# A two-layer transformer on one core: block 0 normalised a layer early, roots moved, logits before results, evictions spread

## The chip, the cores and the metric

The kernel runs on one core of a Trainium2 chip. The core has TensorE (PE, matrix products; PEld are its weight loads), VectorE (DVE), ScalarE (ACT), GpSimd (POOL) and SyncE (SP, which here only issues DMAs). Each engine works through its own queue in order; engines wait for one another by semaphores. The metric is device time in microseconds (us), the median of three runs.

## The reference, cut to what matters

The input x has 4 sequences of 512 tokens with 256 features. Two layers follow, each with attention and a feed-forward part; each part gets a layernorm of x and is added to x.

```python
x = x + attn0(layernorm(x))   # 16 heads of 16, causal, softmax over 512 keys
x = x + ffn0(layernorm(x))    # every output feature picks 2 of 8 experts
x = x + attn1(layernorm(x))   # 16 query heads, 4 kv heads of 128
x = x + ffn1(layernorm(x))    # 4-bit weights, gelu gate, 256 -> 2048 -> 256

def ffn0(h):                                  # h: tokens x 256
    logits = (h @ router_w.T + router_b)      # tokens x 256 x 8
    w, sel = top_k(softmax(logits), 2); w = w / w.sum()
    c = zeros(tokens, 8).at[sel].add(w)       # expert weights, summed over features
    out = einsum('th,eoh->teo', h, expert_w) + expert_b
    return einsum('te,teo->to', c, out)
```

attn1 sees the reshaped array as a sequence axis of 4 and a batch of 512, so its scores are small; four groups of kv heads share the queries four to one. ffn1 unpacks two 4-bit codes from each byte, looks up their values and multiplies by a scale for 32 of them.

## The kernel before, in words

The 2048 tokens lie in SBUF as 16 groups of 128 (`xres`), four groups making a block; there are four blocks. All products are in fp32; a product of 512 columns over 256 features is four matmul instructions.

**The planner.** The order on PE, DVE and POOL is the program's order (in layer 1 that of ACT too; in layer 0 a scheduler orders ACT by its own estimate). The program finds the order as it is written: work off the main line is held in `streams`, generators that yield `need(engine, cost, gap, cond)` before each piece. Between pieces of the main line, `fill` (L140) opens a *slot*: it gives PE and DVE budgets in estimated us, first issues what was deferred, then goes through the streams from the front and lets each issue pieces while the engine's budget is above zero, its condition holds and `gap` slots have passed since its last piece. `defer` (L134) puts off an ACT instruction to the next slot, so that it stands behind other work.

**Layer 0** (the first 421 us). Attention runs in 32 batches: scores, maxima on DVE, a shift of the queries, exponentials on ACT, mixing, and a division (`divided`, L731) with two transposes and two output products per block. Two slots per batch are filled with streams: the norm and projections of the next block (`prepare`), and the feed-forward part. That part has, per group: four *logit* products (`logit_pieces`, L298), 17 steps of *weights* on DVE with a tanh and sums on ACT (`weight_pieces`, L371; the tanh and its follower are `lesser`, L404), four *result* products (`result_pieces`, L318) whose outputs ACT multiplies by the expert weights, and *additions* to `xres` on DVE (`addition_pieces`). `hidden_pieces` (L281) normalises and transposes a block for them. Logits and results are let through by how far the weights are (`made()`). The streams stand in the order fold, additions, weights, results, logits. About half of the feed-forward part of layer 0 is left when layer 1 starts, and is filled into layer 1's attention.

**A norm** (`norm_pieces`, L187) takes statistics of four groups on DVE, an inverse square root by a guess on DVE and ten small steps (`rsqrt_steps`) on POOL or DVE, and writes the normalised `xn` on DVE; where POOL makes the steps, `xn` is held back two slots. Only one norm is under way at a time (`normed`). Four transposes per half follow on PE, and ACT copies them to `xT`.

**Layer 1's attention** (from 421 us). `wqkv` and `wpj` are loaded on SP's queue when layer 0's memory is free. `start_pieces(j)` (L908) normalises block j, transposes it and makes the values; block 0's must be complete before the first round, the others are streams. A round p takes one kv head of one block: five projections (`project1`, four of queries and one of keys), scores, softmax on DVE, `mix` (L999: values mixed, four accumulators copied to `oT` by ACT), four output products `output` (L1017). The rounds are interleaved: the projections of round p+1, with mixing of round p ahead of the third, then the outputs of p with scores and softmax of p+1 between. After each piece `between` (L1070) fills a slot. Its PE budget follows `share`, the layer-0 products still left spread over the slots up to round 8; from round 9 it is 0.2.

```python
def between(dve=None):
    fill(PE=1.9 * share + 0.2, DVE=dve or 2.7 * share + 1.4)
...
for h in range(HPK + 1):
    if h == 2 and p >= 0:
        mix(p)
    if new:
        project1(p + 1, h)
        between()
```

PE's small outputs share two PSUM buffers (`ps_dn`, tag `dn`): projections, products, transposes, values. Each is free again when ACT has copied it.

Once layer 0's last addition is issued, 4-bit weights are unpacked by `dequant_pieces` (L833) in the remaining rounds: DVE steps, and two ACT instructions, `over` (L855) and `sign` (L860).

**Layer 1's feed-forward part** (from about 883 us) is untouched by the change.

Of the kernel before, what the change touches and what calls it, by code (L numbers as in the profile page):

```python
# [32 lines left out]
def tile_transformer(  # L33
# [97 lines left out]
    streams = []  # L131
    deferred = []

    def defer(emit):  # L134

        deferred.append((slot, emit))

    left = {"PE": 0.0, "DVE": 0.0}

    def fill(**budget):  # L140

        nonlocal slot
        slot += 1
        while deferred and deferred[0][0] < slot:
            deferred.pop(0)[1]()
        for engine, b in budget.items():
            left[engine] = min(left[engine], 0.0) + b
        again = True
        while again:
            again = False  # L150
            for stream in list(streams):
                while stream.ready(left):
                    engine, cost = stream.go()
                    left[engine] -= cost
                    again = True
                if stream.next is None:
                    streams.remove(stream)
# [26 lines left out]

    normed = []

    def norm_pieces(j, pool, small, out, deinterleave=False, eng=None, cond=None):  # L187

        yield need("DVE", 1.0, cond=lambda: not normed and (cond is None or cond()))
        normed.append(j)  # L190
        st = small.tile([P, 4, 6], F32, tag="ln_st", name=f"ln_st{j}")
        mv = small.tile([P, 4, 2], F32, tag="ln_mv", name=f"ln_mv{j}")
        rs = small.tile([P, 4], F32, tag="ln_rs", name=f"ln_rs{j}")
        for t in range(4):
            if t == 2:
                yield need("DVE", 1.0)
            nc.vector.bn_stats(st[:, t, :], xres[:, 4 * j + t, :])
            nc.vector.bn_aggr(mv[:, t, :], st[:, t, :])
        eng = eng or nc.gpsimd
        yield need("DVE", 0.6 if eng is nc.gpsimd else 2.6)  # L200
        v = rsqrt_guess(rs, mv[:, :, 1], small, j)
        rsqrt_steps(eng, rs, v, small, j)
        xn = pool.tile([P, 4, HID], F32, tag="xn", name=f"xn{j}")
        for t in range(4):
            if t % 2 == 0:
                yield need("DVE", 0.9, 2 if not t and eng is nc.gpsimd else 0)
            src, dst = xres[:, 4 * j + t, :], xn[:, t, :]
            if deinterleave:
                src = src.rearrange("p (k two) -> p two k", two=2)
                dst = dst.rearrange("p (two k) -> p two k", two=2)  # L210
            nc.vector.tensor_scalar(
                dst, src, mv[:, t, 0:1], rs[:, t : t + 1], ALU.subtract, ALU.mult
            )
        out.append(xn)
# [66 lines left out]
    def hidden_pieces(b):  # L281

        out = []
        done = (4 * b - 5, 1)
        yield from norm_pieces(b, b1, b2, out, cond=lambda: b < 2 or done in halves)
        xT = b2.tile([P, 2, 512], F32, tag="xT", name=f"xT{b}")
        for hc in range(2):
            yield need("PE", 0.5, 1 - hc)
            ps = transposed(out[0], hc, ps_dn, "dn", f"xT_ps{b}_{hc}")
            ps = ps.rearrange("p t q -> p (t q)")  # L290
            if hc:
                nc.scalar.activation(xT[:, hc, :], ps, AF.Identity, bias=last_16)
            else:
                nc.scalar.copy(xT[:, hc, :], ps)
        normed.clear()
        xTs[b] = xT
# [74 lines left out]
    def weight_pieces():  # L371

        tt, stt = nc.vector.tensor_tensor, nc.vector.scalar_tensor_tensor
        for g in range(NT):
            yield need("DVE", 1.25, cond=lambda: g in logits and logits[g][1] < slot)
            d = logits[g][0]
            hi4 = b1.tile([P, 4, HID], F32, tag="hi4", name=f"hi4_{g}")
            lo4 = b1.tile([P, 4, HID], F32, tag="lo4", name=f"lo4_{g}")
# [1 line left out]
            gap = b1.tile([P, HID], F32, tag="gap", name=f"gap_{g}")  # L380
            th = b1.tile([P, HID], F32, tag="th", name=f"th_{g}")
            w1 = b1.tile([P, HID], F32, tag="w1", name=f"w1_{g}")
            c1 = b2.tile([P, NE], F32, tag="c1", name=f"c1_{g}")
            sums = b2.tile([P, NE + 1], F32, tag="sums", name=f"sums_{g}")

            tt(hi4, d[:, 0:4], d[:, 4:8], ALU.max)
# [17 lines left out]
            def lesser(th=th, gap=gap, w1=w1):  # L404
                nc.scalar.activation(th, gap, AF.Tanh, scale=0.5)
                nc.scalar.activation(w1, th, AF.Identity, bias=half_t, scale=0.5)

            defer(lesser)
            for e in (0, 4):
                yield need("DVE", 1.25)  # L410
                tt(  # L411
# [3 lines left out]

            yield need("DVE", 0.7, 1)
            owing = b5.tile([P, HID], F32, tag="owing", name=f"owing_{g}_")
            nc.vector.tensor_scalar(gap, gap, 0.0, -1.0, ALU.is_equal, ALU.mult)  # L420
            stt(owing, th, -1.0, gap, ALU.add, ALU.add)
# [19 lines left out]
            stt(c1, sums[:, :NE], 0.5, c1, ALU.mult, ALU.add)  # L441
            weights[g] = c1, slot
            del logits[g]

# [6 lines left out]
    with ExitStack() as l0:  # L451
# [333 lines left out]
        for piece in prepare(0):  # L785
# [3 lines left out]
        mask(0)  # L789
        fold = Stream(fold_pieces())  # L790
        streams += [
            fold, Stream(addition_pieces()), Stream(counted(weight_pieces())), Stream(result_pieces()),
            Stream(logit_pieces()),
        ]
        for n in range(NBT):
            j, s, gs = batches[n]
# [28 lines left out]
            if n in (2, 6):  # L825
                load_x(n // 4 + 2)
        mixed(NBT - 1)
        last = Stream(divided(*batches[NBT - 1][:2]))
        streams.insert(0, last)
        while last.next is not None:  # L830
# [2 lines left out]
    def dequant_pieces(pool, once, n, packed, scales, to, defer=defer):  # L833

        wi = pool.tile([P, 2, HID], I32, tag="dq_w", name=f"dq_w{n}")
        sc = pool.tile([P, 2, HID], F32, tag="dq_s", name=f"dq_s{n}")
        for i in range(2):  # L840
            nc.sync.dma_start(out=wi[:, i], in_=packed[i])
            for b in range(8):
                nc.sync.dma_start(out=sc[16 * b : 16 * b + 16, i], in_=scales[i](b))
        mi = once.tile([P, 2, 2, HID], I32, tag="dq_m", name=f"dq_m{n}")
        si = once.tile([P, 2, 2, HID], I32, tag="dq_i", name=f"dq_i{n}")
        a = once.tile([P, 2, 2, HID], F32, tag="dq_a", name=f"dq_a{n}")
        over = once.tile([P, 2, 2, HID], F32, tag="dq_b", name=f"dq_b{n}")
# [7 lines left out]
        defer(lambda: nc.scalar.activation(over, mi, AF.Relu, bias=minus_12, scale=2.0))  # L855
        yield need("DVE", 0.9)
        ts(si[:, :, 0], wi, 8, None, ALU.bitwise_and)
        ts(si[:, :, 1], wi, 4, 8, ALU.logical_shift_right, ALU.bitwise_and)

        defer(lambda: nc.scalar.activation(sign, si, AF.Identity, bias=half_t, scale=-0.125))  # L860
        yield need("DVE", 1.25)
        stt(a, mi, 4.0, mi, ALU.max, ALU.add)
        yield need("DVE", 1.25, 1)
        stt(a, a, -4.0, over, ALU.add, ALU.add)
        yield need("DVE", 1.25)
        tt(a, a, sign, ALU.mult)
        yield need("DVE", 1.3)
        tt(to, a, sc.unsqueeze(2).to_broadcast([P, 2, 2, HID]), ALU.mult)
# [16 lines left out]
    with ExitStack() as l1:  # L885
# [14 lines left out]
        def into_T(out, to, name):  # L900

            for hc in range(2):
                yield need("PE", 0.5, 1 - hc)
                ps = transposed(out[0], hc, ps_dn, "dn", f"{name}_ps{hc}")
                nc.scalar.copy(to[:, hc, :], ps.rearrange("p t q -> p (t q)"))
            normed.clear()

        def start_pieces(j):  # L908

            out = []  # L910
            yield from norm_pieces(j, c1, c1, out, cond=lambda: (4 * j + 3, 1) in added)
            xT = c2.tile([P, 2, 512], F32, tag="xT", name=f"xT1_{j}")
            yield from into_T(out, xT, f"xT1_{j}")
            v = c2.tile([P, 4, NKV, P], F32, tag="v", name=f"v{j}")
# [84 lines left out]
        def mix(p):  # L999
# [10 lines left out]
                    )  # L1010
            oT = c2.tile([P, HPK, 512], F32, tag="oT", name=f"oT{p}")
            oq = oT.rearrange("p h (t c q) -> p c t h q", c=NC, q=32)
            for c in range(NC):
                nc.scalar.copy(oq[:, c], avs[c])
            state["o"] = oT

        def output(p, t):  # L1017

# [54 lines left out]
        for p in range(-1, NP):  # L1073
# [22 lines left out]
            for h in range(HPK + 1):  # L1096
                if h == 2 and p >= 0:
                    mix(p)
                    if not new:
                        first_products()  # L1100
                if new:
                    project1(p + 1, h)
                    between()
            for t in range(4):
                if p >= 0:
# [20 lines left out]
    with ExitStack() as f1:  # L1126
# [9 lines left out]
        def inner(j):  # L1136
            xT = normed_T(j, d2, d2, ps_dn, "dn", deinterleave=True) if j else x_first
            it = d2.tile([P, NJ, 2, 512], F32, tag="it", name=f"it{j}")
            for jj in range(NJ):
# [21 lines left out]
                if j < 2 and jj % 4 == 3:  # L1161
                    at = 4 * j + 2 * (jj // 4)
                    for _ in dequant_pieces(
                        d2, d1, f"d{at}", [down_w[at + i] for i in range(2)],
                        [
                            lambda b, i=i: down_s[at + i, b : b + 1, :].to_broadcast([16, HID])
                            for i in range(2)
                        ],
                        wd[:, at : at + 2], lambda emit: emit(),
                    ):  # L1170
                        pass
            return it
# [85 lines left out]
```

## Time and profile before

| what | value |
|---|---|
| median of three runs | 1235.4 us (1234.69 to 1236.05) |
| profiled execution | 1231.27 us, span 1229.6 us |
| mean granted TensorE clock | 0.983 |
| PE busy | 1172.0 us (95%), 7278 matmuls |
| DVE busy | 812.5 us (66%), 1862 instructions |
| ACT busy | 483.7 us (39%), 1101 instructions |
| POOL busy | 131.3 us (11%), 249 instructions |
| DMA | 26.78 MB |

The profile is of one execution, a little faster than the median of the three runs. Busy PE time is modelled from pipelined matmuls and overstates the work, so a stall is better read from the starts of neighbouring groups of matmuls. In a line of the timeline stand: start, duration, engine, line and operation, the names written and read, shapes, count, and in brackets the idle time before it with what ended that. "lg_ps" is a logit product, "eo" a result product, "qk_ps" a projection, "xT_ps" a transpose, "v_ps" a value product, "a" the mixing of layer 1, "o" in L1025 its output product, "th" the tanh of the weights.

### The profile page before, as it was taken

To read this page: it belongs to the slowest core of one execution; us is meant where nothing else is said; L and a number is where in the kernel's file an instruction comes from. 1 tells how busy PE (TensorE), PEld (TensorE's weight loads), DVE (VectorE), ACT (ScalarE), POOL (GpSimd) and SP (SyncE) were. 2 spreads that over 40 slices of the span, in tenths; PEclk is the share of its full clock that TensorE was granted. 3 is DMA by queue.
4 is the path that set the end of the run, shared out by engine and by line. 5 is a ranking of instruction groups with operands and counts; after the bars stand their busy time and mean duration, and the time that the engine had idled before them with its cause. 6 is when DMAs were issued, how large, how long until landed. Compare 5 with 4: busy or idle time off the path is not lost.

```text
span 1229.6 us, 18921 instructions
## 1 busy us (share of the span) xinstructions
PE 1172.0 (95%) x7278; PEld 682.0 (55%) x7278; DVE 812.5 (66%) x1862; ACT 483.7 (39%) x1101; POOL 131.3 (11%) x249
## 2 busy tenths in 40 slices
PE   6888999999999897999999999999999999999998
PEld 3666555555545443555555555555645456475487
DVE  3655589887889838395967396588589962734710
ACT  1243455555555533344444344345234431312300
POOL 7343422111121001000000000100000000000000
PEclk9899999999999988999999999999999999999999
DMA  6031102000000310000000001011010000000000
GB/s 201 5 100 35 19 1 36 1 1 2 1 2 2 117 55 1 1 1 1 1 1 1 1 1 35 10 43 53 1 50 19 1 1 17 1 1 18 0 1 35
DMA packets 19386, 26.78 MB, mean 22 GB/s; under 512 B 4992, under 2 KB 13440, under 8 KB 19040
## 3 DMA queue, kind: packets, MB, share of 16 engines
q1 hardware_dynamic: 18624, 24.40, 7.0%
q10 hardware_dynamic: 672, 1.18, 0.4%
q8 instruction: 57, 0.93, 0.3%
q14 instruction: 33, 0.27, 0.1%
HBM read 19.27 MB, written 2.10 MB: 17 GB/s over the span
## 4 chain that ended last, share of the span: by engine, by line
PE 77%; DVE 16%; ACT 3%; DMA 2%; issue 1%; POOL 1%; SPq 0%; ACTq 0%; DVEq 0%; POOLq 0%
PE qk_ps L937 10%; PE y L1178 9%; PE g L874 9%; PE u L874 9%; PE o L1025 8%; PE lg_ps L251 7%; PE eo L251 6%; PE s L633 4%; DVE mx L653 3%; PE s L683 2%; PE v_ps L919 2%; PE qk_ps L548 2%; PE av L719 2%; PE s L950 1%; DVE lg L411 1%
## 5 line engine op out<-in xcount | busy, mean ns | idle before, releaser
L937 PE MATMUL qk_ps<-xT,wqkv 128*128 128x512 f32 x320 | 151.3, 604 | 5.0 <-ACT qT L941 5.0
L251 PE MATMUL lg_ps<-rw,xT 128*128 128x512 f32 x256 | 125.7, 614 | 4.4 <-ACT part L339 1.4
L251 PE MATMUL eo<-ew,xT 128*128 128x512 f32 x256 | 122.8, 605 | 1.9 <-ACT part L339 1.9
L1025 PE MATMUL o<-wpj,oT 128*128 128x256 f32 x512 | 119.4, 382 | 0.0
L653 DVE TENSOR_REDUCE mx<-s 128x1 f32<-128x384 f32 (+3 forms) x176 | 100.4, 632 | 18.3 <-PE s L648 18.3
L1178 PE MATMUL y<-wd,it 128*128 128x256 f32 x512 | 112.1, 379 | 0.0
L1025 PEld LDWEIGHTS o<-wpj,oT 128*128 128x128 f32 x512 | 96.0, 190 | 28.2 <-issue 16.4
L1178 PEld LDWEIGHTS y<-wd,it 128*128 128x128 f32 x512 | 97.0, 190 | 15.6 <-issue 2.9
L937 PEld LDWEIGHTS qk_ps<-xT,wqkv 128*128 128x128 f32 x320 | 59.7, 192 | 75.3 <-issue 61.8
L692 ACT ACTIVATE pt<-s 128x512 f32<-128x512 f32 (+1 forms) x176 | 83.7, 561 | 35.7 <-PE s L683 35.6
L874 PE MATMUL g<-xT,wgu 128*128 128x512 f32 x192 | 90.5, 593 | 0.0
L874 PE MATMUL u<-xT,wgu 128*128 128x512 f32 x192 | 90.2, 592 | 0.0
L702 POOL TENSOR_SCALAR_AFFINE_SELECT pt<-pt 128x256 f32<-128x256 f32 (+2 forms) x88 | 56.7, 651 | 267.1 <-ACT pt L692 266.7
L339 ACT ACTIVATE part<-eo,c 128x256 f32<-128x256 f32 x128 | 53.7, 472 | 78.9 <-PE eo L251 78.9
L1156 ACT ACTIVATE th<-sq 128x512 f32<-128x512 f32 x64 | 40.3, 630 | 88.6 <-DVE sq L1155 88.6
L251 PEld LDWEIGHTS eo<-ew,xT 128*128 128x128 f32 x256 | 47.6, 193 | 48.5 <-issue 40.9
L251 PEld LDWEIGHTS lg_ps<-rw,xT 128*128 128x128 f32 x256 | 46.7, 194 | 49.8 <-issue 38.4
L633 PE MATMUL s<-qk 32*128 32x128 f32 (+3 forms) x512 | 67.0, 496 | 2.6 <-ACT pt L692 1.9
L239 DVE TENSOR_TENSOR xres<-xres,y 128x256 f32<-128x256 f32 x16 | 6.7, 420 | 91.3 <-PE y L1178 91.3
L313 ACT COPY lg<-lg_ps 128x512 f32<-128x512 f32 x64 | 37.7, 589 | 71.2 <-PE lg_ps L251 71.2
L366 DVE TENSOR_TENSOR part<-part 128x512 f32<-128x512 f32 x32 | 21.9, 684 | 65.5 <-ACT part L339 65.4
L941 ACT COPY qT<-qk_ps 128x512 f32<-128x512 f32 x64 | 37.8, 593 | 61.4 <-PE qk_ps L937 61.4
(254 smaller groups left out, 1820.2 us busy)
## 6 DMA issues: line engine op xcount, KB each, us to landing
qk<-stage SPq DMA_DIRECT2D x56, 64.0 KB, 2.4
wqkv<-in_w_qkv SPq DMA_DIRECT2D x2, 1536.0 KB, 8.3
rw<-in_router_w SPq DMA_DIRECT2D x8, 256.0 KB, 4.6
ew<-in_expert_w SPq DMA_DIRECT2D x8, 256.0 KB, 4.8
wpj<-in_w_proj SPq DMA_DIRECT2D x1, 2048.0 KB, 15.4
out<-xres SPq DMA_DIRECT2D x4, 512.0 KB, 2.6
xres<-in_x SPq DMA_DIRECT2D x3, 512.0 KB, 7.1
dq_wgu<-in_gate_w SPq DMA_DIRECT2D x8, 128.0 KB, 2.4
```

What stands on the lines that cost most here:

```text
L251: nc.tensor.matmul(ps, lhsT=xT[:, hc, (g % 4) * P : (g % 4 + 1) * P], rhs=w[:, hc, 2 * pair : 2 * pair + 2, :].rearrange("p e o -> p (e o) ...
L339: nc.scalar.mul(part[:, e % 4], ps[:, i], c[:, e : e + 1])
L633: nc.tensor.matmul(tiles[h][:, b * nk : (b + 1) * nk].rearrange("p (c k) -> p c k", k=P), lhsT=queries(j, g)[r, s], rhs=qk[r, g, : j + 1, ...
L653: nc.vector.tensor_reduce(maxes[n % 2][:, :nb, h, 0], ps[:, : nb * nk].rearrange("p (b k) -> p b k", b=nb), AX.X, ALU.max,)
L692: nc.scalar.activation(pt[:, i, : nb * nk], tiles[2 * pair + i][:, : nb * nk], AF.Exp, scale=0.25)
L702: nc.gpsimd.affine_select(out=last, in_=last, compare_op=ALU.is_ge, fill=0.0, base=0, pattern=pattern, channel_multiplier=-1,)
L874: nc.tensor.matmul(ps, lhsT=wgu[:, w, half, jj, par * P : (par + 1) * P], rhs=xT[:, half, :], start=half == 0, stop=half == 1,)
L937: nc.tensor.matmul(ps, lhsT=wqkv[:, hc, kv, h, :], rhs=xT[:, hc, :], start=hc == 0, stop=hc == 1,)
L941: nc.scalar.copy(kT if h == HPK else qT[:, h, :], ps)
L1025: nc.tensor.matmul(ys[t // 2][:, t % 2], lhsT=state["o"][:, h, t * P : (t + 1) * P], rhs=wpj[:, HPK * kv + h, :], start=kv == 0 and h == 0 ...
L1156: nc.scalar.activation(th, sq, AF.Tanh, scale=0.7978845608028654)
L1178: nc.tensor.matmul(ps, lhsT=it[:, c // 2, c % 2, t * P : (t + 1) * P], rhs=wd[:, c // 2, c % 2, :], start=c == 0, stop=c == 2 * NJ - 1,)
```

## The change

- Deferral gets a number of slots (one, as before, by default). The tanh of the weights and the `sign` of the dequantisation are deferred by two. The weights' next step waits until the tanh has been issued, the multiplication by `sign` waits a slot.
- In the streams, logits stand in front of results. The weights of group g wait for the results of group g-5; their outputs `c1` have five buffers instead of two.
- Layer 0's norm of block 3 (`hidden_pieces`) makes its roots on DVE, and its first transpose waits two slots after `xn` instead of one.
- Layer 1's norm of block 0 is issued in layer 0's tail, with the roots on DVE; layer 1 begins with its transposes, two slots later. The other blocks of layer 1 keep their roots on POOL; `xn` is held back three slots, the first transpose two.
- Of the four copies of mixing to `oT`, one follows mixing and one each of the three projections after it (in the last round all four follow mixing).

```diff
-    def defer(emit):
-        deferred.append((slot, emit))
+    def defer(emit, slots=1):
+        deferred.append((slot + slots, emit))
...
-        while deferred and deferred[0][0] < slot:
-            deferred.pop(0)[1]()
+        for due in [d for d in deferred if d[0] <= slot]:
+            deferred.remove(due)
+            due[1]()
...
-    def norm_pieces(j, pool, small, out, deinterleave=False, eng=None, cond=None):
+    def norm_pieces(j, pool, small, out, deinterleave=False, eng=None, cond=None, wait=2):
...
-                yield need("DVE", 0.9, 2 if not t and eng is nc.gpsimd else 0)
+                yield need("DVE", 0.9, wait if not t and eng is nc.gpsimd else 0)
...
-        yield from norm_pieces(b, b1, b2, out, cond=lambda: b < 2 or done in halves)
+        last = b == NBLK - 1
+        yield from norm_pieces(
+            b, b1, b2, out, eng=nc.vector if last else None,
+            cond=lambda: b < 2 or done in halves,
+        )
...
-            yield need("PE", 0.5, 1 - hc)
+            yield need("PE", 0.5, 0 if hc else 1 + last)
...
-            yield need("DVE", 1.25, cond=lambda: g in logits and logits[g][1] < slot)
+            yield need(
+                "DVE", 1.25,
+                cond=lambda: g in logits and logits[g][1] < slot
+                and (g < 5 or (g - 5, 1) in halves),
+            )
...
-            c1 = b2.tile([P, NE], F32, tag="c1", name=f"c1_{g}")
+            c1 = b5.tile([P, NE], F32, tag="c1", name=f"c1_{g}")
...
                 nc.scalar.activation(th, gap, AF.Tanh, scale=0.5)
                 nc.scalar.activation(w1, th, AF.Identity, bias=half_t, scale=0.5)
+                lessers.append(th)
-            defer(lesser)
+            defer(lesser, 2)
...
-            yield need("DVE", 0.7, 1)
+            yield need("DVE", 0.7, 1, cond=lambda: lessers)
+            lessers.clear()
...
-            fold, Stream(addition_pieces()), Stream(counted(weight_pieces())), Stream(result_pieces()),
-            Stream(logit_pieces()),
+            fold, Stream(addition_pieces()), Stream(counted(weight_pieces())),
+            Stream(logit_pieces()), Stream(result_pieces()),
...
         mixed(NBT - 1)
+        streams.insert(0, Stream(norm_pieces(0, b1, b2, normed_first, eng=nc.vector)))
         last = Stream(divided(*batches[NBT - 1][:2]))
...
-        defer(lambda: nc.scalar.activation(sign, si, AF.Identity, bias=half_t, scale=-0.125))
+        defer(lambda: nc.scalar.activation(sign, si, AF.Identity, bias=half_t, scale=-0.125), 2)
...
-        yield need("DVE", 1.25)
+        yield need("DVE", 1.25, 1)
         tt(a, a, sign, ALU.mult)
...
-                yield need("PE", 0.5, 1 - hc)
+                yield need("PE", 0.5, 0 if hc else 2)
...
-            out = []
-            yield from norm_pieces(j, c1, c1, out, cond=lambda: (4 * j + 3, 1) in added)
+            out = [] if j else normed_first
+            if j:
+                yield from norm_pieces(
+                    j, c1, c1, out, cond=lambda: (4 * j + 3, 1) in added, wait=3
+                )
...
-            for c in range(NC):
-                nc.scalar.copy(oq[:, c], avs[c])
             state["o"] = oT
+            state["a"] = [lambda c=c: nc.scalar.copy(oq[:, c], avs[c]) for c in range(NC)]
+
+        def mixed_out(n):
+            for _ in range(n):
+                state["a"].pop(0)()
...
                     mix(p)
+                    mixed_out(1 if new else NC)
                     if not new:
                         first_products()
                 if new:
                     project1(p + 1, h)
+                    if h >= 2 and p >= 0:
+                        mixed_out(1)
                     between()
```

More of the change, by code (lines that the diff above doesn't have):

```diff
@@ L373, in weight_pieces @@
         tt, stt = nc.vector.tensor_tensor, nc.vector.scalar_tensor_tensor
+        lessers = []
         for g in range(NT):
-            yield need("DVE", 1.25, cond=lambda: g in logits and logits[g][1] < slot)
+            yield need(
[3 more added lines that the diff above has]
+            )
             d = logits[g][0]
@@ L443, in weight_pieces @@
             del logits[g]
+    normed_first = []
     with ExitStack() as l0:
@@ L1168, in inner @@
                         ],
-                        wd[:, at : at + 2], lambda emit: emit(),
+                        wd[:, at : at + 2], lambda emit, slots=1: emit(),
                     ):
```

## The prediction

> **What bounds the kernel now.** First the kernel by stage: busy time of each engine in five stretches (columns: stretch and length in us; busy time and count of PE, PEld, DVE, ACT, POOL; granted PE clock, DMA share, GB/s).
>
> ```profile
> 0.00:421.00 421.00, 385.37 (x3986) 228.36 (x3986) 307.54 (x744) 193.69 (x486) 115.29 (x189) 0.98 0.12 30
> 421.00:492.00 71.00, 59.50 (x194) 26.83 (x193) 44.10 (x133) 27.72 (x66) 8.12 (x30) 0.88 0.20 73
> 492.00:732.00 240.00, 239.76 (x1129) 134.54 (x1128) 157.51 (x389) 106.24 (x280) 2.02 (x10) 1.00 0.00 1
> 732.00:883.00 151.00, 144.86 (x859) 88.17 (x858) 107.23 (x216) 64.42 (x123) 5.89 (x20) 0.99 0.11 29
> 883.00:1229.60 346.60, 342.55 (x1117) 204.09 (x1115) 196.13 (x383) 91.62 (x146) 0.00 (x0) 1.00 0.04 13
> ```
>
> From 492 us on TensorE is the bound: four matmuls of 128x512 (one "product") take 1.72 us wherever nothing disturbs them, and almost nothing is lost. PE's work is the same after the change, so only its lost time can move. I measure a loss as start of a group to start of the next, less the undisturbed time (1.72 us a product, 0.86 us for 8 transposes). Layer 0 loses most, but VectorE's chain of maxima under a fixed budget paces it. What the change touches are single stalls; next the waits of PE that name most of them, then, from the timeline, the seam between the layers, with the landing times of layer 1's weights:
>
> ```profile
> PE xT_ps L227 <- DVE xn L211: 7.8, 3, 3.2
> PE qk_ps L937 <- ACT qT L941: 5.0, 6, 2.1
> ```
>
> ```profile
> 419.84 0.82 SPq L890 DMA_DIRECT2D wqkv<-in_w_qkv  x2
> ...
> 430.83 1.38 DVE L211 TENSOR_SCALAR xn<-xres,ln_mv,ln_rs 128x256 f32<-128x256 f32 x4 [1.22 <-POOL ln_rs L183]
> 431.39 1.76 PE L227 MATMUL xT_ps<-ident,xn 128*128 128x128 f32 x8 [1.84 <-DVE xn L211]
> ...
> 434.72 5.68 PE L919 MATMUL v_ps<-wqkv,xT 128*128 128x512 f32 x7 [1.56 <-ACT xT L905]
> ```
>
> ```profile
> DMA to landing us min/median/max: 6.6/8.3/10.0
> ```
>
> PE waits for a normalised block, then for its copies; the second half of the weights lands at 420.2 + 10.0 = 430.2, unnoticed. Next ScalarE as the culprit (timeline, then clock by stretch):
>
> ```profile
> 735.68 1.88 PE L251 MATMUL eo<-ew,xT 128*128 128x512 f32 x4
> ...
> 736.22 0.42 ACT L405 ACTIVATE th<-gap 128x256 f32<-128x256 f32 x1 [2.77 <-DVE gap L401]
> ...
> 737.08 2.03 ACT L1014 COPY oT<-a 128x512 f32<-128x512 f32 x4
> ...
> 738.98 0.62 ACT L941 COPY qT<-qk_ps 128x512 f32<-128x512 f32 x1
> ...
> 739.65 3.50 PE L937 MATMUL qk_ps<-xT,wqkv 128*128 128x512 f32 x4 [2.09 <-ACT qT L941]
> ```
>
> ```profile
> 735.70:744.90 9.20, 7.11 (x14) 2.79 (x13) 8.57 (x26) 5.80 (x17) 0.00 (x0) 0.81 0.00 0
> 786.00:793.00 7.00, 5.27 (x16) 2.42 (x15) 3.08 (x4) 4.38 (x8) 3.13 (x7) 1.00 0.00 1
> ```
>
> A tanh that waits for VectorE and four mixing copies stand in front of the copy PE needs. Last, what follows a round's fifth projection today:
>
> ```profile
> 857.68 1.89 PE L1025 MATMUL o<-wpj,oT 128*128 128x256 f32 x8
> ...
> 857.88 0.59 ACT L941 COPY kT<-qk_ps 128x512 f32<-128x512 f32 x1 [1.59 <-PE qk_ps L937]
> 858.36 1.15 ACT L855 ACTIVATE dq_bgu<-dq_mgu,minus 128x1024 f32<-128x1024 int32 x1
> ```
>
> The output products o start with no gap, because the oT copies were done long before. The next ACT instruction starts 0.48 us after the kT copy.
>
> **The change part by part.**
>
> *A. Block 0 normalised in layer 0's tail.* Loss at the seam: 427.67 to 431.39 less 1.72 is 2.0; transposes 431.39 to 434.72 less 0.86 is 2.5; values 434.72 to 444.10 less 6.88 is 2.5 (clock 0.74 there): 7.0. After, three products precede the transposes instead of five (two slots instead of a whole norm), so they stand at 426.0, and the values want both weight halves: SP still issues them behind layer 0's last o (L764), so they land at 430.2. The values end at 430.2+0.86+5.16, plus one half-clock stretch (1.7) for an idle PE: 438.0 against 444.1, with 2 products (3.4) still to do. Gain 2.7; ends 0 (a longer half clock) and 4.4 (none). The norm's 6 us on DVE (4 x 0.59 statistics, 0.6 guess, 10 x 0.16 roots, 4 x 0.35) take slots that the weights had; DVE even idles 3.3 us there before the add at 406.2. Without that cover the divisions of the tail would come up to 2 us later. Its ten POOL roots leave POOL.
>
> *B. Block 3 of layer 0, roots on DVE, transposes a slot later.* Loss 461.36 to 465.65 less 0.86, 465.65 to 467.53 less 0.86, 467.53 to 470.72 less 1.72: 3.4+1.0+1.5 = 5.9. All roots now lie on the queue that also writes xn, and two slots (3.4 us each here) cover the rest. Gain 5.5 (ends 0, 5.9).
>
> *C. Later blocks of layer 1, one slot more before xn and before the transposes.* Block 1: 477.33 to 483.75 less 3.44, then 2.4 and 1.85: 7.2. POOL's chain (478.64 to 483.16) gets a slot more. Gain 6.5 (ends 0, 7.2).
>
> *D. Tanh two slots later, in layer 1.* 735.68 to 739.65 less 1.72 is 2.25; the next product at half clock loses 1.57. Gain 3.8 (ends 0, 3.8). Behind the new wait stand the owing step and all later DVE work; the steps before it end about 5 us after the tanh today in layer 0, a slot is 3.7 us, so I add nothing (at most the 0.93 us of both activations in 16 groups, were the cover gone).
>
> *E. The same in layer 0.* The tanhs at 240.11 and 312.93 (2.3 and 2.8 us of waiting) hold back the exponentials whose score buffers PE wants: 2.70 and 2.75 us for 8 score matmuls against 1.07 at 272.02. That is 3.3; I take 3.0, as ACT's order in layer 0 is set elsewhere (ends -2, 3.9).
>
> *F. Dequantisation's sign later, evictions interleaved.* Stalls after 780: 787.03 to 789.36 (1.9), the values at 802.7 (1.6), two of 0.4. I take 2.5 of 4.3 (ends 0, 4.3); the copies stay on ACT.
>
> *G. Mixing's evictions spread.* In place of four oT copies after mixing comes one, then one after each of the projections 2, 3 and 4. The o products need all four (each copy carries a quarter of the queries of every o), and the last is now behind the kT copy, which waits for projection 4. From 857.68: kT copy from 857.88, oT from 858.36 to 858.96, and weights to load again (0.19): 1.4 us in which PE has nothing, where today it has no gap. A product in the slot between (1.72) hides it. In rounds 9 to 14 PE's budget is 0.2 a slot, so all six pay, less half a round for transposes or values that fall there. In rounds 0 to 8 that slot has no product in four of today's nine (after 585.9, 649.1, 712.5 and 744.9); once only results are left, each pair of them waits a slot for its addition, so two slots of six are empty. A part of those four may fill: I take 8 rounds in all, 11.2. Ends: 4 rounds x 1.2 = 4.8, and 15 x 1.4 = 21 plus half clocks.
>
> *H. Logits in front.* Results fall up to five groups behind the weights. Block 3's norm waits for the results of group 7 and blocks 1 and 2 of layer 1 for the sums of 7 and 11, so block 2 of layer 1 comes late, when only results are left to cover it: cost 2.0 (0 to 5). DVE works on weights without a break (26 us of waiting between 442.1 and 468.5 go) and may hold up softmax: 1.0 (0 to 4). In layer 0 the weights follow each other within 0.2 us except at 340 and 411, so the order of products gains nothing there.
>
> Sum: 2.7+5.5+6.5+3.8+3.0+2.5 = 24.0 gained, 11.2+2.0+1.0 = 14.2 lost, net 9.8. The profiled execution took 1231.3 (span 1229.6, 1.7 around it), so 1221.5; it lies 4.1 under the median of 1235.4, so I predict **1225.6**.
>
> A rule against the rows. The profile grants half clock after the 2.09 us gap at 737.6 (0.81 over the stretch) and full clock after 1.73 us at 787.6. So G's 1.4 us should leave the clock alone, but a round with 0.7 more would cost another 1.7. The Trainium skill, "TensorE: Matmul & The Clock Gate", Part 1, says that the clock falls to half after at least one idle window of about 3.4 us. By that no G stall could ever cost clock and the sum would stay at 9.8; by the rows, six such rounds would take 6 x 2.4 = 14 and turn it round.
>
> **The rivals.**
>
> *Other side: G decides.* All fifteen rounds pay (21.0), and in the six late ones a dequantisation (1.15 us) stands in front of kT, so the gap passes 2.09 and the clock halves: 6 x 2.4 = 14.4. 24.0-3.0-35.4 = -14.4: 1250. It decides from 15 rounds at 1.4 us on, or 9 at 2.4. For it: the six late rounds have nothing between. Against: today's dequantisations fall behind kT (858.36).
>
> *The seams stay.* Results lag, so the late norms are awaited elsewhere (B and C give nothing) and A meets the weights' landing: 24.0-14.7-14.2 = -4.9: 1240. For it: the 430.2. Against: two slots are at least 3.4 us, the longest wait was 3.2.
>
> *The spread is covered.* Only four rounds pay 1.2: 24.0-4.8-3.0 = 16.2: 1219. For it: products follow projection 4 in five of today's nine rounds.
>
> **How the numbers follow.** Forecast 0.46 (its own range 1217 to 1234, from G at 6 to 12 rounds and C or D missing), covered spread 0.16, seams stay 0.18, G decides 0.20. 0.2% is 2.5 us, about what three rounds tell from no change. Faster: 0.44+0.16+0.02 = 0.62. Same: 0.02+0.08 = 0.10. Slower: 0.08+0.20 = 0.28. The range takes in the covered spread with A and F at their ends (1213) and half of G's case (1245).
>
> **What would show it.** Right: waits of o L1025 (or its weight loads) on oT L1014, about 1.2 to 1.4 us each, absent before; v_ps L919 waiting for the wqkv DMA near 430; no xT_ps wait over 1 us at 460 to 490; th L405 with no idle before it. Wrong: o without waits; xT_ps still waiting for xn; half clock in rounds 9 to 14; layer 0's end moved by more than 4 us from 419.6.

## The result, and the profile after

The changed kernel takes 1247.4 us (median of 5 runs, 1241.8 to 1248.6) against 1235.4 us before: a ratio of 1.0107, with a 95% interval of 1.0088 to 1.0125. It is 1.1% slower. Forecast were 1225.6 us and faster. The profiled execution took 1247.4 us with a span of 1245.5 us, 15.9 us more than the span before (the medians differ by 12.0 us). PE's work is the same, and its lost time, read from the starts of its groups as in the prediction, is larger by the same 15.9 us, so the whole of it can be looked for among PE's stalls. First the changed kernel by stage (columns as in the prediction):

```profile
0.00:426.00 426.00, 386.58 (x3977) 230.79 (x3978) 307.67 (x759) 191.28 (x480) 117.51 (x189) 0.96 0.12 29
426.00:497.00 71.00, 63.98 (x244) 29.60 (x243) 53.76 (x142) 34.17 (x97) 0.00 (x0) 0.98 0.21 75
497.00:741.00 244.00, 232.23 (x1069) 127.29 (x1068) 158.43 (x417) 103.95 (x272) 5.34 (x20) 0.99 0.00 1
741.00:890.00 149.00, 141.08 (x817) 84.53 (x815) 94.46 (x176) 60.76 (x104) 5.27 (x20) 1.00 0.11 29
890.00:1245.50 355.50, 350.32 (x1177) 210.31 (x1176) 199.93 (x391) 92.76 (x149) 0.00 (x0) 1.00 0.04 12
```

Layer 0 ends about 5 us later, at a lower clock (0.96 against 0.98); the 71 us after it hold more of PE's work than before (64.0 us busy against 59.5, clock 0.98 against 0.88); and the stretch that was full before now has PE idle for 12 us. The waits of PE give the names (what waited, for what, us in total, times, longest):

```profile
PE o L1046 <- ACT oT L1032: 9.3, 8, 1.5
...
PE xT_ps L228 <- ACT part L344: 6.5, 2, 6.0
PE eo L252 <- ACT lg L318: 4.0, 4, 2.2
PE eo L252 <- ACT xT L299: 3.3, 1, 3.3
...
PE lg_ps L252 <- DVE sm L977: 1.9, 1, 1.9
...
PE v_ps L937 <- DMA wqkv<-in_w_qkv: 1.8, 1, 1.8
```

The 7.8 us in which transposes waited for `xn` and the 5.0 us in which projections waited for a query copy are no longer among the large ones. In their place stand the output products o behind `oT` (term G), a transpose that waits 6 us for ScalarE's result multiplications, a result product that waits for the copies of a transposed block, and a softmax.

**A round with spread copies.** From the timeline, ACT in a late round and the output products that follow:

```profile
866.33 0.59 ACT L1032 COPY oT<-a 128x512 f32<-128x512 f32 x1
...
868.00 0.59 ACT L1032 COPY oT<-a 128x512 f32<-128x512 f32 x1
868.48 1.16 ACT L875 ACTIVATE dq_cgu<-dq_igu,half_t 128x1024 f32<-128x1024 int32 x1
869.52 0.59 ACT L959 COPY qT<-qk_ps 128x512 f32<-128x512 f32 x1
869.99 0.61 ACT L1032 COPY oT<-a 128x512 f32<-128x512 f32 x1
870.95 0.59 ACT L959 COPY kT<-qk_ps 128x512 f32<-128x512 f32 x1 [0.35 <-PE qk_ps L955]
871.43 0.59 ACT L1032 COPY oT<-a 128x512 f32<-128x512 f32 x1
872.08 1.99 PE L1046 MATMUL o<-wpj,oT 128*128 128x256 f32 x8 [1.16 <-ACT oT L1032]
```

```profile
867.00:880.00 13.00, 11.84 (x73) 8.08 (x72) 7.55 (x13) 4.41 (x8) 0.00 (x0) 1.00 0.00 1
```

The fourth oT copy stands behind the kT copy, which waits for the fifth projection; the output products start 1.16 us late. The clock stays at 1.00 (the column after POOL's). Six of the eight such waits lie in the rounds after 780 us; the others are at 559 and 631 us.

**Layer 0, block 2's norm.** From the timeline at 353 to 377 us:

```profile
353.64 0.42 ACT L439 ACTIVATE spare<-owing__4016 128x256 bf16<-128x256 f32 x1 [1.33 <-DVE sums L434]
...
354.74 2.04 ACT L706 ACTIVATE pt<-s 128x512 f32<-128x512 f32 x4
355.37 3.04 PE L647 MATMUL s<-qk 32*128 32x512 f32 x6 [0.82 <-ACT pt L706]
...
370.91 1.37 DVE L212 TENSOR_SCALAR xn<-xres,ln_mv,ln_rs 128x256 f32<-128x256 f32 x4
...
372.31 1.10 PE L228 MATMUL xT_ps<-ident,xn 128*128 128x128 f32 x8
...
374.15 2.04 ACT L706 ACTIVATE pt<-s 128x512 f32<-128x512 f32 x4
376.06 0.61 ACT L299 COPY xT<-xT_ps 128x512 f32<-128x512 f32 x1
376.52 0.73 ACT L297 ACTIVATE xT<-xT_ps,last 128x512 f32<-128x512 f32 x1
376.72 3.66 PE L252 MATMUL eo<-ew,xT 128*128 128x512 f32 x4 [3.31 <-ACT xT L299]
```

In the kernel before, the same `xn` stands 28 us earlier:

```profile
342.91 1.37 DVE L211 TENSOR_SCALAR xn<-xres,ln_mv,ln_rs 128x256 f32<-128x256 f32 x4
```

This norm may not start before the second half of the results of group 3 (`done` in `hidden_pieces`), and results now come later. Its copies now meet four exponentials on ACT, and PE stops for 3.3 us. Some 20 us ahead, sums of the weights on ACT stand in front of exponentials that scores wait for. After both stops the products run at half clock (four matmuls in 3.66 us in place of 1.88).

**Layer 1, block 3's norm.** From the timeline:

```profile
533.91 1.88 PE L955 MATMUL qk_ps<-xT,wqkv 128*128 128x512 f32 x4
...
537.95 1.38 DVE L212 TENSOR_SCALAR xn<-xres,ln_mv,ln_rs 128x256 f32<-128x256 f32 x4
539.25 0.68 DVE L371 TENSOR_TENSOR part<-part 128x512 f32<-128x512 f32 x1
539.97 0.42 DVE L372 TENSOR_TENSOR part<-part 128x256 f32<-128x256 f32 x1
540.42 0.42 DVE L373 TENSOR_TENSOR xres<-xres,part 128x256 f32<-128x256 f32 x1
...
540.94 0.84 ACT L344 ACTIVATE part<-eo,c 128x256 f32<-128x256 f32 x2 [7.96 <-DVE xres L373]
...
541.67 0.59 ACT L959 COPY qT<-qk_ps 128x512 f32<-128x512 f32 x1
...
541.83 1.97 PE L228 MATMUL xT_ps<-ident,xn 128*128 128x128 f32 x8 [6.04 <-ACT part L344]
```

A softmax, the whole norm and an addition are in one line on VectorE; ScalarE's result multiplications wait 7.96 us for that addition, the query copy stands behind them, and PE has no `dn` buffer left for 6 us (the program gives it two). Before the change this norm's `xn` started 73 us earlier:

```profile
465.10 1.37 DVE L211 TENSOR_SCALAR xn<-xres,ln_mv,ln_rs 128x256 f32<-128x256 f32 x4
```

### The profile page after: what moved, and what is told of

Read it like the earlier page. It is cut to its first block, busy times and chain, and to the rows that moved or that the text cites. A ratio compares the mean times of both kernels' runs of the same rounds, so it can differ in the third digit from the quotient of the medians.

```text
span 1245.5 us, 18945 instructions
## 1 busy us (share of the span) xinstructions
PE 1174.2 (94%) x7278; PEld 682.5 (55%) x7278; DVE 814.2 (65%) x1882; ACT 482.9 (39%) x1101; POOL 128.1 (10%) x229
## 4 chain that ended last, share of the span: by engine, by line
PE 74%; DVE 18%; ACT 4%; DMA 2%; issue 2%; SPq 0%; ACTq 0%; DVEq 0%
PE y L1202 9%; PE qk_ps L955 9%; PE g L889 9%; PE u L889 9%; PE o L1046 7%; PE eo L252 7%; PE lg_ps L252 6%; PE s L647 4%; DVE mx L667 3%; PE s L697 2%; PE qk_ps L562 2%; PE av L733 2%; DVE lg L422 1%; PE a L1026 1%; PE v_ps L937 1%
## 5 line engine op out<-in xcount | busy, mean ns | idle before, releaser
L683 DVE TENSOR_TENSOR qk<-qk,mxT 128x128 f32<-128x128 f32 (+2 forms) x44 | 15.2, 346 | 75.2 <-PE mxT L678 75.2
```

## The experiments

Ratios are to the kernel before, with 95% intervals; 0.001 is 1.2 us. The first four separate the spread copies from the order of the streams.

**All four copies after mixing again**

```diff
-                    mixed_out(1 if new else NC)
+                    mixed_out(NC)
...
-                    if h >= 2 and p >= 0:
-                        mixed_out(1)
```

> The changed kernel with all four mixing copies straight after mixing, as before. Theory 1 (the last copy behind the keys' copy costs about 1.4 us in eight rounds): the waits of the output products on oT vanish and the time falls by 10 to 12 us, from about 1247 to about 1236. Theory 2 (the order of logits and results and the later work on VectorE carry the loss): it falls by less than 4 us, and the stalls at 460 to 475 and 533 to 547 stay as they are. Rival: the burst brings back a stall in front of a query copy as at 737 before, 4 us, and the gain is under 8.

Measured: 1.0019 (1.0010 to 1.0028), 10.8 us less than with spread copies. No wait of o on oT is left among PE's waits; these two are:

```profile
PE xT_ps L228 <- ACT part L344: 6.4, 2, 5.9
PE eo L252 <- ACT xT L299: 3.3, 1, 3.3
```

So the spread costs what term G said, and the two norms' stalls are another matter.

**Results in front of logits again, copies spread**

```diff
-            Stream(logit_pieces()), Stream(result_pieces()),
+            Stream(result_pieces()), Stream(logit_pieces()),
```

> The changed kernel with results again in front of logits in the streams; all else as changed. Theory 2: the VectorE backlog behind softmax (6 us at 460 to 475) and the late norm of block 3 (9 us at 533 to 547) go, and layer 0's tail ends 4 to 8 us earlier: 1247 falls to 1226 to 1234. Theory 1 alone: no more than 4 us, since the oT waits stay.

Measured: 0.9960 (0.9948 to 0.9972), some 18 us less than the changed kernel. The waits on oT stay (9.6 us, 8 times); the single stops of 3.3 us at 373, 2.2 us at 470 and 6.0 us at 536 us are gone. This is the larger of the two harms.

**Both undone**

> Both undone: four copies after mixing, and results in front of logits; the moved norm, the roots, the later tanh and the later sign stay. If the two theories add up: 1215 to 1224, faster than before by 1 to 1.5 per cent. If the rest of the change is itself harmful (roots on VectorE, later tanh): 1232 or more.

Measured: 0.9895 (0.9880 to 0.9910). The rest of the change gains 13 us. In this arrangement the spread costs 0.9960 less 0.9895, 8 us, and the order 1.0019 less 0.9895, 15.3 us.

**The kernel before with the spread alone**

The `mixed_out` edits of the change, and nothing else.

> The kernel before with nothing changed but the spread of the mixing copies. Theory 1: waits of the output products on oT in six late rounds and in two to four of the others, plus 8 to 14 us, less 4 us for the stall at 735 to 743: 1240 to 1246. Rival (the spread is covered by products and norms): within 3 us of before.

Measured: 1.0092 (1.0079 to 1.0105), 11.3 us; o waits ten times for oT, 12.0 us in all. PE's program in layer 0 is that of the kernel before here, and yet its lost time up to the last o of layer 0 was 4.7 us larger in the profiled execution, and that o started 4.5 us later: so much can one stretch scatter, and differences of a few us in one stretch of two single traces are read with that in mind.

**Spread, but ahead of each projection**

```diff
+                    if h >= 2 and p >= 0:
+                        mixed_out(1)
                     project1(p + 1, h)
-                    if h >= 2 and p >= 0:
-                        mixed_out(1)
```

and results in front of logits.

> Results in front of logits again, and the evictions still spread, but each of the three later oT copies is issued in front of the projection it used to follow, so that the last one stands in front of the kT copy and not behind it. Theory (place in the queue is what the spread costs): no wait of o on oT, and none of the 6.3 us in which qk_ps waits for a qT copy behind a burst of four: 0.985 of the kernel before (0.982 to 0.989), under the burst's 0.9895. Rival (spreading itself costs, since copies among the projections hold back the qT copies that PE needs): qk_ps waits grow, 0.990 to 0.996.

Measured: 0.9875 (0.9859 to 0.9892). Against the same kernel with the copies behind the projections (0.9960) this is 10 us less, for moving each copy by one place. o waits 0.8 us in all, as the theory said; but projections still wait 4.0 us for query copies (6.3 us with the burst), and the time isn't told apart from the burst's (0.9895). The stall that it should have cured, a query copy behind a dequantisation and a burst, as in the kernel with both parts undone,

```profile
772.23 1.15 ACT L870 ACTIVATE dq_bgu<-dq_mgu,minus 128x1024 f32<-128x1024 int32 x1 [4.09 <-DVE dq_mgu L869]
773.29 2.03 ACT L1032 COPY oT<-a 128x512 f32<-128x512 f32 x4
775.18 1.10 ACT L959 COPY qT<-qk_ps 128x512 f32<-128x512 f32 x2
775.85 3.64 PE L955 MATMUL qk_ps<-xT,wqkv 128*128 128x512 f32 x4 [3.60 <-ACT qT L959]
```

is shorter with it (2.65 us in place of 3.60) but not gone, since ACT idles 4.11 us for VectorE's `dq_mgu` ahead of it.

**Logits in front, alone**

The swap of the two streams, the bound of five groups and the five `c1` buffers, in the kernel before.

> The kernel before with logits in front of results alone (with the bound of five groups and the five c1 buffers that belong to it). Theory 1 (the order harms by itself: results late, VectorE in one long run of weights): 1.008 to 1.015, a late norm of block 3 after 500 us. Theory 2 (it harms only together with the norms that the change moved to VectorE): 0.998 to 1.004, no stall over 3 us between 500 and 600.

Measured: 0.9970 (0.9957 to 0.9984): a gain, a little better than theory 2 had it. Theory 1 fell, though block 3's norm does come after 500 us (`xn` at 533.9). The order harms only with other parts of the change.

**Block 3's roots on POOL**

```diff
-            b, b1, b2, out, eng=nc.vector if last else None,
+            b, b1, b2, out,
```

once with results in front and once with logits in front, both with the burst of copies.

> Mixing's copies in one burst, results in front of logits, and the roots of layer 0's block 3 back on POOL; the extra slot before its transposes stays. Theory (the slot is worth it, the engine is not): 0.9895 plus or minus 0.001, no loss over 2 us at block 3's transposes. Rival (the engine is what gains, term B of the prediction): 0.993 to 0.995, a wait of xT_ps for xn of 3 us or more.

> Mixing's copies in one burst, logits in front of results as in the changed kernel, and the roots of layer 0's block 3 back on POOL. Theory (its norm on VectorE, standing in front of the additions, makes the 6 us stall near 534): 0.994 to 0.998, and no wait of xT_ps for part. Rival (results that come late make that norm late, whichever engine has the roots): 1.000 to 1.004 as with the roots on VectorE (1.0019), a stall of 5 us or more between 525 and 550.

Measured: 0.9869 (0.9852 to 0.9886), and 1.0077 (1.0061 to 1.0092). With results in front the move of the roots gains nothing; that the extra slot covers POOL's chain is likely, but the slot alone was not undone. And with logits in front VectorE's roots aren't what makes the stall of layer 1: with the roots on POOL one of 4.2 us stays at the same place,

```profile
535.67 3.18 PE L252 MATMUL eo<-ew,xT 128*128 128x512 f32 x4 [4.19 <-ACT part L344]
```

and the whole is 7 us slower still, so this theory fell too. In the traces that slowness lies after 600 us, in waits for query and value copies between 770 and 840 us; why they come was not traced.

**Single terms undone** (from the kernel with burst and results in front, 0.9895)

Block 0's norm back in layer 1:

```diff
-        streams.insert(0, Stream(norm_pieces(0, b1, b2, normed_first, eng=nc.vector)))
...
-            out = [] if j else normed_first
-            if j:
+            out = []
```

the tanh after one slot:

```diff
-            defer(lesser, 2)
+            defer(lesser)
```

and layer 1's later norms with their old slots:

```diff
-                    j, c1, c1, out, cond=lambda: (4 * j + 3, 1) in added, wait=3
+                    j, c1, c1, out, cond=lambda: (4 * j + 3, 1) in added
...
-                yield need("PE", 0.5, 0 if hc else 2)
+                yield need("PE", 0.5, 1 - hc)
```

> Burst of copies and results in front of logits (0.9895 with all else of the change), and block 0 of layer 1 normalised in layer 1 again. If term A is worth its 2.7 us: 0.9917 (0.990 to 0.993), and a loss of 4 us or more between the last o of layer 0 and the values, in place of about 2. Rival (the landing of the weights takes it all back): 0.9895 plus or minus 0.001.

> Burst and results in front of logits, and the tanh one slot after its gap, as before the change. If terms D and E are worth what the prediction gave them (3.8 and 3.0 us): 0.995. If only D is there, since layer 0's loss up to its last o did not change with the tanh's delay (20.9 us against 20.1 before): 0.9925. If neither: 0.9895 plus or minus 0.001.

> Burst and results in front of logits, and the later norms of layer 1 and their transposes one slot earlier, as before the change. If term C is worth its 6.5 us: 0.995, with losses of 2 to 3 us at the transposes between 475 and 490. Rival (with other spacing the norm finds cover anyway): 0.9895 plus or minus 0.001.

Measured: 0.9898 (0.9880 to 0.9915), 0.9883 (0.9864 to 0.9903), 0.9864 (0.9843 to 0.9885). None of the three is worth anything by itself in the total; with C undone the kernel is, if anything, 4 us faster. Of term A the seam does show its price (loss between the last o of layer 0 and 500 us 13.2 us in place of 9.0), but the loss after 600 us is 16.2 us in place of 19.6.

**Two good variants together, and three**

The copies ahead of their projections, results in front and block 3's roots on POOL (the edits above); then with layer 1's later norms at their old slots too.

> Results in front of logits, copies spread but each ahead of its projection, and the roots of layer 0's block 3 on POOL: the two best variants together. If their gains add (0.9875 and 0.9869 against 0.9895): 0.985 (0.983 to 0.987), no wait of o on oT over 1 us. Rival (both take the same loss away, or none): 0.987 to 0.989.

> Results in front of logits, copies spread ahead of their projections, block 3's roots on POOL, layer 1's norms at their old slots: each of these alone gave 0.9864 to 0.9875 against 0.9895. If any of it adds: 0.983 to 0.986. Rival (stalls near 768 and beyond take back what the seam gains): 0.986 to 0.989.

Measured: 0.9877 (0.9857 to 0.9897), and 0.9896 (0.9882 to 0.9910). Single gains don't add. The best kernels of the study lie at 0.986 to 0.988 and aren't told apart.

**All norms as before, with either order**

Terms A, B and C undone together (the edits of A and C above, the roots on POOL, and the line below), burst of copies, tanh and sign late as changed.

```diff
-            yield need("PE", 0.5, 0 if hc else 1 + last)
+            yield need("PE", 0.5, 1 - hc)
```

> Burst and results in front of logits, and all of terms A, B and C undone together: block 0 normalised in layer 1, block 3 of layer 0 with its roots on POOL and no extra slot, layer 1's norms one slot earlier. Undone one by one, A and C moved the time by less than 0.4%. Theory (together they are the gain, since the loss at the seam fell from 22.5 to 9.0 us with them): 0.999 (0.997 to 1.001), seam loss 20 us or more. Rival (the gain comes from what is left: five c1 buffers, later tanh and sign): 0.993 or below.

> The same with logits in front of results. Theory (logits in front is harmful through the moved norms, whose VectorE work falls into the slot of a softmax and in front of an addition): 0.997 to 1.000, as with logits in front alone (0.997), no stall over 4 us between 520 and 550. Rival (it is the later tanh, whose wait holds VectorE's steps back): 1.002 to 1.006, with the stall.

Measured: 0.9947 (0.9933 to 0.9962) with results in front, 0.9939 (0.9927 to 0.9951) with logits in front. The first lies between its theory and its rival: the moved norms are about half of the 1.05% gained, and the rest comes from the buffers, the later tanh and the later sign together. So the moved norms gain 0.5% with results in front and lose 0.8% with logits in front (1.0019), and the order costs nothing without them. With the tanh at its old slot and the norms moved,

> Burst, logits in front of results, all norms as changed, the tanh one slot after its gap again. Theory (moved norms): 1.002 as with the later tanh, the stall of 6 us near 534 remains. Rival (later tanh): 0.997 or below, no stall over 4 us between 520 and 550.

the ratio is 1.0036 (1.0023 to 1.0049) and the stall near 534 remains (5.9 us of waiting): it is the norms as moved, not the tanh. PE's lost time, by the prediction's method, in one profiled execution of each (us; "seam" from the last o of layer 0 to 500 us; the differences between rows are what counts):

| norms | in front | 340 to last o | seam | 500 to 600 | from 600 | ratio |
|---|---|---|---|---|---|---|
| kernel before | results | 20.1 | 22.5 | 2.3 | 19.7 | 1 |
| as before | results | 21.5 | 22.1 | 2.3 | 14.0 | 0.9947 |
| as before | logits | 27.1 | 14.6 | 3.0 | 12.9 | 0.9939 |
| moved | results | 20.9 | 9.0 | 2.3 | 19.6 | 0.9895 |
| moved | logits | 28.1 | 11.8 | 12.8 | 14.1 | 1.0019 |

Logits in front delay block 2's norm in layer 0 (`xn` at 369 to 372 us in place of 341 to 344) and cost 6 to 7 us there, with either norms. They also delay block 3's norm out of the seam, which takes 7.5 us of the seam's loss away as long as the seam has it. The moved norms take that same loss away. With both, the gain is had only once, and the delayed norm meets a softmax and the additions between 500 and 600 us. Being late isn't enough for that stall: with the norms as before and logits in front block 3's norm is nearly as late,

```profile
533.14 1.38 DVE L212 TENSOR_SCALAR xn<-xres,ln_mv,ln_rs 128x256 f32<-128x256 f32 x4
```

and only 3.0 us are lost in that stretch. Which of the moved norms, or of their slots, makes the stall was not tried by itself.

**The order in one layer only** (norms moved, burst; results or logits in front at first)

```diff
         mixed(NBT - 1)
+        streams[-1], streams[-2] = streams[-2], streams[-1]
```

> Burst, all norms as changed, results in front of logits up to the last mixing of layer 0, logits in front from there on. Theory (7 to 8 us of the harm arise in layer 0, where block 2's norm waits for late results; the rest in layer 1): loss between 340 us and the last o of layer 0 of 21 us as with results in front, and 0.994 to 0.997, between 0.9895 (results in front all along) and 1.0019 (logits in front all along). Rival (the harm in layer 1 is inherited from late results of layer 0): 0.989 to 0.991, no stall over 4 us between 500 and 600.

> The reverse: logits in front in layer 0, results in front from the last mixing of layer 0 on. Theory (two separate harms): loss of 28 us between 340 us and the last o, and 0.994 to 0.998. Rival (late results of layer 0 carry on): 1.001 to 1.003, the stall near 534 remains.

Measured: 0.9914 (0.9898 to 0.9930) with logits in front in layer 1 only, 0.9984 (0.9971 to 0.9998) in layer 0 only. From 340 us on the loss before the last o is 20.6 and 26.8 us, as expected. But the times are not what the stalls suggest. The order in layer 0 costs 0.9% (11 us). The traces place 6 us of that between 340 us and the last o and 3 to 4 us at the seam. In layer 1 it costs 0.2%, which is not told apart from nothing, although the stall there (5.7 us of waiting, and 13.4 us lost between 500 and 600) is the largest of that layer: the loss after 600 us is 13.8 us in place of 19.6 with it. So a harm in layer 0 is shown in the time; that of layer 1 is seen in its stall, and mostly made up for later.

## Why the prediction was wrong

**G was right**, in place, mechanism and size. Forecast were 8 rounds at 1.4 us, 11.2; the trace has 8 waits of 1.16 us on average, six of them in the late rounds as said, and undoing the spread gives 10.8 us. The copy ahead of its projection, which takes the wait and 10 us away, shows that the place behind the kT copy is the cause. The clock didn't fall, so the rival "G decides", which gave nearly the measured time (1250), was not what happened; its number is near by luck.

**H was the step that failed.** It put logits in front at 2.0 + 1.0 us; beside the moved norms they cost 15.3 us. The sentence that went wrong is that in layer 0 "the order of products gains nothing there": it was read as no effect, but results that come later hold back block 2's norm by 28 us, and its copies then stand behind exponentials. The order in layer 0 alone costs 11 us, of which the traces show 6 there. The sign of it that the prediction named, an end of layer 0 more than 4 us from 419.6, is there (the last group of output products starts at 423.1 us in place of 417.8), but it is a weak one: the run with the spread alone, whose layer 0 is unchanged, has 422.3. In layer 1 the prediction names block 3's norm among those that wait for results, but puts the lateness on block 2 of layer 1 alone; it is block 3's norm that comes 73 us later and stalls.

**B, C and A** were right as readings of the seam: with results in front its loss falls from 22.1 to 9.0 us, 13.1 against a forecast of 14.7, and the values wait for the weights' landing (1.8 us) as A said. Two things were wrong beside it. B's roots on VectorE gain nothing over POOL's with results in front; whether it is B's slot that gains was not tried alone. And the gain isn't kept: 5.6 us come back after 600 us, so that the moved norms gain 6.4 us in time. Why is open.

**D and F**: forecast 6.3 us, and with the old norms the loss from 600 us falls from 19.7 to 14.0, 5.7 us. In layer 1 of the changed kernel the idle time in front of a tanh falls from 11.9 us (6 times) to 0.3 us (once). That these two terms earned the 5.7 us is likely but not shown: with the moved norms the tanh one slot earlier changes nothing (0.9883 against 0.9895), the sign was never undone by itself, and the five buffers changed with them.

**E was wrong**, 3.0 us forecast and nothing found: in layer 0 ACT idles 13.5 us in front of 7 tanhs before, and just as much with the tanh deferred by two slots and old norms. That fits the prediction's own remark that ACT's order in layer 0 is set elsewhere, by a scheduler, which a deferral in the program's order need not bind; it should have lowered E.

The sum: with the five buffers A to F keep 13 us of the 24 forecast, H takes 15.3 and G 10.8, 13 us slower in all. (These are the steps from the kernel before over two of the runs to the changed kernel, so they add up to the measured difference by themselves.) With H alone set right the forecast would have been 1238. So there were two misses of the same sign: norms made late, and gains of A to F that didn't add.

## What to carry to other kernels

Before an order is changed, list every condition that waits for the work that becomes later, and find where each released piece will then stand in the in-order queues; a price for "a bit later" without that place is a guess. Two edits that cure the same stall aren't worth their sum, and the gain from a cured stall can be lost again later, as it was here after 600 us: undo the edits in pairs, not only singly. A copy that is the last of several inputs of a product belongs ahead of the copy that waits for a later product: moving it by one place was worth 10 us here.

## What was not expected of the hardware

The granted clock can halve after a shorter stop than the 2.09 us that the prediction went by, and the length of the stop does not settle it. PE idles 0.82 us before the score matmuls at 355.37; then (columns as above, the clock after POOL)

```profile
350.00:354.00 4.00, 3.99 (x71) 2.42 (x69) 3.93 (x12) 1.47 (x5) 0.00 (x0) 1.00 0.00 0
354.00:358.00 4.00, 3.17 (x8) 1.08 (x6) 2.29 (x9) 2.87 (x9) 0.82 (x2) 0.78 0.01 4
358.00:362.00 4.00, 4.00 (x10) 1.75 (x9) 3.08 (x9) 0.00 (x0) 0.00 (x0) 0.50 0.00 0
```

the clock is at half. The 1.16 us of the round shown above left it at 1.00, as did 1.73 us in the kernel before (786 to 793 in the prediction). In the long stop of layer 1 it falls while PE is still without work, which comes back at 541.83:

```profile
536.00:540.00 4.00, 0.00 (x0) 0.00 (x0) 3.62 (x16) 0.00 (x0) 0.00 (x0) 1.00 0.00 0
540.00:544.00 4.00, 1.97 (x8) 1.57 (x8) 3.93 (x17) 3.06 (x11) 0.00 (x0) 0.57 0.00 0
```

The clock's own record in the traces shows a pattern: half clock begins at 356.22, 376.70 and 540.54 us in the changed kernel, which are 6 and 48 times 3.41 us apart, and it lasts 6.83, 3.41 and 6.83 us. In all 20 traces the clock changes only at such multiples of 3.41 us. So where a stop falls between these points may count beside its length; that was not tried. The Trainium skill, "TensorE: Matmul & The Clock Gate", Part 1, gives an idle window of about 3.4 us as the condition for half clock; by the profile PE was busy for 2.56 of the 3.4 us before 356.22, so this trace shows half clock without an idle window.

What stays open is why the loss after 600 us is 5 to 6 us smaller with logits in front in layer 1, or with the old norms, than with moved norms and results in front (all with the later tanh); with logits in front and block 3's roots on POOL it is not smaller. That dequantisations then meet other rounds is seen in the traces, but was not tried by itself.
